# Three small edits to a two-layer graph kernel: a bias row's load behind x1's squares, one code step per tile step, and layer 0's slope on ScalarE

## The chip, the cores and the metric

The kernel runs on one core of one Trainium2 chip. The metric is the device time of one execution in microseconds (us); lower is better. A core has TensorE (PE, matmuls; its weight loads are listed as PEld), VectorE (DVE), ScalarE (ACT), GpSimd (POOL) and SyncE (SP). [...] Transfers are issued from the queues of SP, POOL and ACT[...].

## The reference

`x` is 4096 x 512, `adj` is a 4096 x 4096 matrix of 0 and 1 (int32).

```python
# layer 0
keep = (A > 0) & (cumsum(A > 0, axis=1) <= 64)        # at most 64 neighbours of a row
cnt  = keep.sum(axis=1, keepdims=True)
nb   = leaky_relu((keep @ X / max(cnt, 1)) @ W_nb.T + b_nb)        # slope 0.01
own  = leaky_relu(X @ W_line.T + b_line)
x1   = layernorm(X + own + where(cnt > 0, nb, 0))
# layer 1
Wh   = x1 @ W + bW
e    = leaky_relu((Wh @ a1 + b1)[:, None] + (Wh @ a2 + b2)[None, :], 0.2)
h    = softmax(where(adj > 0, e, -9e15), axis=1) @ Wh
out  = layernorm(x1 + h)
```

## The kernel before, in words

The 4096 rows are 32 blocks ("tiles") of 128. There is no scheduler: the order of the program's calls is the order in each engine's queue. Four stages follow each other.

**Stage 1** (L393 on) makes `y = X @ W_nb.T` (kept in SBUF as `y_hi + y_lo`) and the `own` part (to DRAM as `own_d`). Beside it run the **codes**: each row block of `adj` is cut in two chunks of 2048 columns, 64 chunks in all. For chunk q, `load_adj` fetches it on SP, `edge` (L167, ACT) turns it to 0/1 flags, `scan` (L179 to L184, DVE) counts down the 64 neighbours, and `pack` (L202 ACT, L203 a transfer on POOL) writes a byte code per edge to DRAM. Buffers of edge and left are two deep, so `edge(q+1)` waits until `scan(q-1)` is through.

**Stage 2** (L494 on) is `keep @ y`. Each of the 32 tiles is done in four steps of 8 blocks, so `s = 4 i + g` runs over 128 steps. One step on PE is 16 matmuls (L509, `y_hi` and `y_lo` in turn). `make_kt(s + 2)` (L249, ACT) unpacks the codes for two steps ahead into one of three `kt` buffers, which means that it waits for step s - 1 on PE. The codes of the second half of `adj` are still made here: `codes_step` at the end of a step starts a scan in 25 of 64 steps, and `codes_late` at the next step issues that chunk's `edge(q+1)` and `pack(q-1)` together.

`finish(i - 1, g)` ends the tile before, one part at each step: g = 0 scales the sum and adds the bias (L468) and applies the slope (L471), both on DVE; g = 1 adds `own` and starts the layer norm (L475, L117 to L126, the power on POOL); g = 2 applies it (L131) and stores x1 (L482); g = 3 makes the two dot products with `wa_rows` (L487).

**Stage 3** (L805 on) is `Wh = x1 @ W`, 32 steps of four matmuls each (L809). x1 comes from DRAM as 32 x 32 squares (`load_turned`, L561, SP) into four slots of the tile `front`, and `turn_x1` (L575, DVE) turns each to the matmul's layout; the first three go to the tile `early`, which lies where `y` lay. `finish_wh` (L584) adds the row `bias_w`; `combine_wh` (L597 to L600) makes sums of Wh that stage 4 wants. Beside it the attention weights of the first two blocks are made (`mask` L621 and L624, `score` L613, `weigh` L666), and `turn` (L685) and `combine` (L698 to L701) make the first two operands of stage 4. Ahead of the loop SP holds, in this order, W's four loads (L542), `bias_w` (L546), four `load_turned`, block 31's `own` (L777), the first `nat` codes (L608), and three more `load_turned`.

**Stage 4** (`consume`, L724) multiplies the weights with Wh by a scheme of seven products of blocks (Strassen), 64 calls over 16 pairs of blocks. Products 1 to 7 of a pair lie two to a PSUM bank, in an order `where` (L708); the very last call alone takes the products in another order (4, 1, 2, 6, 7, 5, 3). After it an epilogue (L876 to L896) joins the products, normalises and stores the last two blocks.

```python
            while late_q:
                q = late_q.pop()
                edge(q + 1)
                pack(q - 1)
...
                nc.vector.scalar_tensor_tensor(t, t, 0.01, t, ALU.mult, ALU.max)
...
    bias_w = ep.tile([P, C], F32, name="res", bufs=1)
    nc.sync.dma_start(bias_w, b_w.partition_broadcast(P))
```

Of the kernel before, what the change touches and what calls it, by code (L numbers as in the profile page):

```python
# [14 lines left out]
AF = mybir.ActivationFunctionType  # L15
ALU = mybir.AluOpType
# [4 lines left out]
P = 128  # L21
# [3 lines left out]
SLOPE = 0.01  # L25
# [7 lines left out]
def two_layer_adj_gnn(  # L33
# [16 lines left out]
    nc = tc.nc  # L50
    N, C = x.shape
    NB = N // P
# [84 lines left out]
    with ExitStack() as l0:  # L137
# [25 lines left out]
        def edge(s):  # L163
            if s < NB * NCH:
                b, h = divmod(s, NCH)
                edge_of[s] = adj_p.tile([P, CH], BF16, name="edge")
                nc.scalar.activation(  # L167
                    edge_of[s], loaded.pop(s), AF.Sigmoid, bias=steep[:, 0:1], scale=STEEP,
                    accum_out=cnts[:, h, b : b + 1],
                )  # L170
# [27 lines left out]
        def pack(s):  # L198
            if 0 <= s < NB * NCH:
                b, h = divmod(s, NCH)  # L200
                code = adj_p.tile([P, CH // 2], BF16, name="code")
                nc.scalar.copy(code.bitcast(U8), seen_of.pop(s))  # L202
                nc.gpsimd.dma_start(code_d[b][:, ts(h, CH // 2)], code)  # L203
# [16 lines left out]

        late_q = []

        def codes_late():

            while late_q:
                q = late_q.pop()
                edge(q + 1)
                pack(q - 1)

        def codes_step(s):  # L230
            while done[0] < min(s, NB * NCH + 1):
                codes_late()
                q = done[0]
                load_adj(q + 2)
                scan(q)
                late_q.append(q)
                done[0] += 1

        KB = 8
# [3 lines left out]
        def make_kt(s):  # L243
            if s < NB * NS:
                b, g = divmod(s, NS)
                if s not in kts:
                    kts[s] = ktb_p.tile([P, KB // 2, 2, P], F32R, name="kt")
                bytes_ = ktbs[b].bitcast(U8)[:, ts(g, KB // 2), :]
                nc.scalar.activation(  # L249
                    kts[s], bytes_.rearrange("p t (i r) -> p t r i", r=2),  # L250
                    AF.Sigmoid, bias=steep[:, 1:2], scale=STEEP,
                )
# [195 lines left out]

        def load_kt(b):
            if b < NB:  # L450
                assert done[0] > NCH * (b + 1) and not late_q
                ktbs[b] = ktb_p.tile([P, NT, P], BF16, name="ktb")
                nc.sync.dma_start_transpose(ktbs[b], code_d[b])

# [2 lines left out]
        def place(name, bufs=2):  # L457
# [2 lines left out]
                return spare.pop(0)  # L460
            return work.tile([P, C], F32, name=name, bufs=bufs)

        def finish(i, g):
            if i < 0:
                return
            if g == 0:
                t = place("t")
                nc.vector.scalar_tensor_tensor(  # L468
                    t, accs.pop(i), rcnt[:, i : i + 1], bias_nb, ALU.mult, ALU.add
                )  # L470
                nc.vector.scalar_tensor_tensor(t, t, 0.01, t, ALU.mult, ALU.max)  # L471
                fin[i] = t
            elif g == 1:
                t, y = fin[i], owns.pop(i)
                nc.vector.scalar_tensor_tensor(  # L475
                    y, t, some[:, i : i + 1], y, ALU.mult, ALU.add
                )
                fin[i] = y, ln_stats(y)
            elif g == 2:
                y, stats = fin[i]  # L480
                ln_apply(y, stats)
                nc.gpsimd.dma_start(x1_blk(i), y)  # L482
            else:
                y, _ = fin.pop(i)
                for k in range(2):
                    junk = place("junk", 1)
                    nc.vector.scalar_tensor_tensor(  # L487
                        junk, y, 1.0, wa_rows[k], ALU.mult, ALU.mult,
                        accum_out=e12[:, 1 - k, i : i + 1],
                    )  # L490
# [3 lines left out]
        for s in range(NB * NS):  # L494
            i, g = divmod(s, NS)
            make_kt(s + 2)
            codes_late()
            if g == 0:
                load_kt(i + 2)
                accs[i] = ps_acc.tile([P, C], F32, name="acc")  # L500
            if g == 2:
                if i < NB - 1:
                    owns[i] = place("own")
                    nc.sync.dma_start(owns[i], own_d[i])
            kt = kts.pop(s)
            for k in range(KB):
                j = g * KB + k
                for term in (y_hi, y_lo):
                    nc.tensor.matmul(  # L509
                        accs[i], kt[:, k // 2, k % 2, :], term[:, j, :],  # L510
                        start=(j == 0 and term is y_hi),
                        stop=(j == NB - 1 and term is y_lo),
                    )
            finish(i - 1, g)
            codes_step(start + int((s + 1) * RATE / NS))

# [24 lines left out]
            ws[ts(n, SQ), :, :], w[ts(n, P), :].rearrange("(m b) c -> b m c", b=SQ)  # L543
        )
    bias_w = ep.tile([P, C], F32, name="res", bufs=1)
    nc.sync.dma_start(bias_w, b_w.partition_broadcast(P))  # L546


    bt = big.tile([P, NS // 2, 7, HC], F32, name="bt")
# [6 lines left out]
    def load_turned(s):  # L556

        if s < NS:
            part = x1_d[s // 8].rearrange("(n s a) c -> s a n c", s=8, a=SQ)[s % 8]
            for n in range(NC):  # L560
                nc.sync.dma_start(  # L561
                    x1s[ts(n, SQ), s % 4, :].rearrange("a (j c) -> a j c", c=P),
                    part[:, :, ts(n, P)],
                )
# [37 lines left out]
    def load_nat(b, h):  # L602

        if b < NB:
            nats[b, h] = ep.tile([P, 2, NS * SQ // 2], BF16, name="nat")
            rows = code_d[b].rearrange("(i a) (n x) -> n a i x", a=SQ, n=4)
            for n in range(4):
                nc.sync.dma_start(nats[b, h][ts(n, SQ)], rows[n][:, ts(h, 2), :])  # L608
# [71 lines left out]
    def turn(q):  # L680

        g, k = divmod(q, NP)
        a = rp.tile([P, 2, 8, P], F32, name="a")
        for r in range(2):
            nc.vector.transpose(  # L685
                a[:, r].rearrange("p s (i a) -> p i s a", a=SQ),
                wts[2 * g + r][:, :, ts(k, 8 * SQ)].rearrange("p i (s x) -> p i s x", x=SQ),
            )
        if k == NP - 1:
            del wts[2 * g], wts[2 * g + 1]  # L690
        parts[q] = a
# [13 lines left out]
        }  # L705


    where = {1: (0, 0), 2: (0, 1), 4: (1, 0), 7: (1, 1), 5: (2, 0), 6: (2, 1), 3: (3, 0)}  # L708

    def consume(q):  # L710
        g, k = divmod(q, NP)
        if k == 0:
            two = [ps_s.tile([P, 2, HC], F32, name="pt")]
            two += [ps_acc.tile([P, 2, HC], F32, name="acc") for _ in range(3)]
            banks[g] = {n: two[i][:, j, :] for n, (i, j) in where.items()}
        part = parts.pop(q)


        order = (1, 2, 4, 7, 5, 6, 3) if q < NP * NT - 1 else (4, 1, 2, 6, 7, 5, 3)
        for n in order:  # L720
            lhs, rhs = part[n]
            mate = [m for m in order if where[m][0] == where[n][0]]
            for j in range(4):
                nc.tensor.matmul(  # L724
                    banks[g][n], lhs[:, j, :], bt[:, 4 * k + j, rhs, :],
                    start=(k == 0 and j == 0 and n == mate[0]),
                    stop=(k == NP - 1 and j == 3 and n == mate[-1]),
                )
# [46 lines left out]
    for s in range(4):  # L775
        load_turned(s)
    nc.sync.dma_start(owns[NB - 1], own_d[NB - 1])  # L777
    load_nat(0, 0)
    load_nat(0, 1)
    for s in range(3):  # L780
        turn_x1(s)
        load_turned(s + 4)
    for g in range(4):
        finish(NB - 1, g)


# [18 lines left out]
    for s in range(NS):  # L805
        pws[s] = ps_acc.tile([P, C], F32, name="acc")
        x1t = x1ts.pop(s)
        for m in range(NC):
            nc.tensor.matmul(  # L809
                pws[s], x1t[:, m, :], ws[:, m, :], start=(m == 0), stop=(m == NC - 1)  # L810
            )
        if s > 0:
            finish_wh(s - 1)
        turn_x1(s + 3)
        load_turned(s + 7)
        if FIRST <= s < FIRST + 8:
            b, i = divmod(s - FIRST, NI)
            mask(b, i)
            score(b, i)
        if FIRST + 4 <= s < FIRST + 12:  # L820
            b, i = divmod(s - FIRST - 4, NI)
            if i == 0:
                greatest(b)
                shift(b)
            weigh(b, i)
        if s in (FIRST + 14, FIRST + 18):
            q = (s - FIRST - 14) // 4
            turn(q)
            combine(q)
        elif s >= FIRST + 8:  # L830
            combine_wh()
    finish_wh(NS - 1)
# [98 lines left out]
```

## Time and profile before

| what | us |
|---|---|
| three runs | 1611.77, 1612.21, 1615.34 |
| median of the runs | 1612.21 |
| the profiled execution, its own time | 1611.63 |
| its span, first to last instruction | 1609.9 |
| stage 1's matmuls begin without a break | 84.4 |
| stage 2's matmuls | 235.7 to 704.2 |
| stage 3's matmuls | 709.7 to 826.1 |
| stage 4's matmuls | 826.1 to 1599.8 |

The profile is of one execution, taken by the hardware profiler. A group's line gives line, engine and operation, what it writes and reads, its shape and count, then the busy time and the mean duration in ns, then the engine's idle time before it and what ended that. The chain of waits follows the last instruction back, at each step to what released it. A timeline lists instructions by start and duration; the bracket behind one is the idle time of its engine before it. The windows view gives the engines' busy time in stretches, and the TensorE clock that was granted as a share of full speed.

### The profile page before, as it was taken

What the parts mean: (1) busy time and instruction counts of PE and PEld (TensorE: products, weight loads), DVE (VectorE), ACT (ScalarE), POOL (GpSimd) and SP (SyncE); (2) the same over time, 40 slices, a digit from 0 to 9 for tenths busy, and PEclk for the clock granted to TensorE, in tenths of its full rate; (3) what the DMA queues carried; (4) which work ended last, traced back from release to release, by engine and by line L of the source; (5) the groups of instructions that cost most, each with busy time, mean ns of one, the idle gap of its engine ahead of it and who ended that gap; (6) DMA issues with size and microseconds to landing.
All of it is one profiled execution on the core that took longest, in us unless ns stands there. A gap on an engine that the chain in (4) does not pass through costs nothing.

```text
span 1609.9 us, 18503 instructions
## 1 busy us (share of the span) xinstructions
PE 1583.8 (98%) x6456; PEld 1221.9 (76%) x6456; DVE 1328.1 (82%) x2186; ACT 903.2 (56%) x1054; POOL 258.1 (16%) x396
## 2 busy tenths in 40 slices
PE   9999999999999999989999999999999999999997
PEld 5444448888888787854468888888888888888886
DVE  4999987999999999845798788888788888788863
ACT  2655556677676766413437655567655567655520
POOL 4455532222122222101000000000000000000000
PEclk9999999999999999999999999999999999999999
DMA  8887868767776676335211111111111111111100
GB/s 199 286 264 232 262 211 239 216 202 212 220 208 198 209 213 193 100 103 118 79 40 27 53 40 53 44 29 46 53 41 53 43 30 47 53 40 53 40 7 33
DMA packets 168365, 192.74 MB, mean 120 GB/s; under 512 B 101408, under 2 KB 134464, under 8 KB 160080
## 3 DMA queue, kind: packets, MB, share of 16 engines
q1 hardware_dynamic: 147968, 131.38, 29.6%
q0 software_dynamic: 19728, 59.27, 10.8%
q8 instruction: 50, 0.82, 0.2%
q10 hardware_dynamic: 576, 0.92, 0.2%
q14 instruction: 43, 0.35, 0.1%
HBM read 132.65 MB, written 42.08 MB: 109 GB/s over the span
## 4 chain that ended last, share of the span: by engine, by line
PE 69%; DVE 23%; DMA 3%; issue 2%; ACT 1%; POOL 1%; SPq 0%; DVEq 0%; POOLq 0%; ACTq 0%
PE acc L724 34%; PE pt L724 14%; DVE left L179 10%; PE acc L340 9%; PE acc L509 9%; PE acc L809 3%; DVE left L184 2%; DVE junk L487 2%; DVE own L475 1%; DVE st L117 1%; DVE t L471 1%; DMA a<-in_adj_dram 1%; DVE t L468 1%; DVE own L131 1%; DVE c L575 1%
## 5 line engine op out<-in xcount | busy, mean ns | idle before, releaser
L509 PE MATMUL acc<-y_hi,kt 128*128 128x512 f32 x1016 | 396.3, 390 | 2.9 <-ACT kt L249 2.9
L509 PE MATMUL acc<-y_lo,kt 128*128 128x512 f32 x1016 | 395.8, 390 | 0.0
L724 PE MATMUL acc<-bt,s 128*128 128x256 f32 x1536 | 342.1, 379 | 0.0
L724 PEld LDWEIGHTS acc<-bt,s 128*128 128x128 f32 x1536 | 292.3, 190 | 39.2
L621 ACT ACTIVATE w<-nat,few 128x1024 f32<-128x1024 uint8 x128 | 136.9, 1135 | 277.1 <-DVE a L685 237.0
L126 POOL TENSOR_TENSOR rs<-ve,few 128x1 f32<-128x1 f32 x64 | 76.1, 1190 | 1021.1 <-DVE ve L124 1021.1
L724 PE MATMUL acc<-bt,a 128*128 128x256 f32 x1024 | 231.6, 379 | 0.0
L724 PE MATMUL pt<-bt,a 128*128 128x256 f32 x1024 | 231.5, 379 | 0.0
L509 PEld LDWEIGHTS acc<-y_hi,kt 128*128 128x128 f32 x1016 | 190.7, 188 | 44.5 <-ACT kt L249 5.0
L509 PEld LDWEIGHTS acc<-y_lo,kt 128*128 128x128 f32 x1016 | 190.9, 188 | 39.3
L724 PEld LDWEIGHTS pt<-bt,a 128*128 128x128 f32 x1024 | 194.9, 190 | 26.5 <-issue 0.5
L724 PEld LDWEIGHTS acc<-bt,a 128*128 128x128 f32 x1024 | 194.9, 190 | 26.1
L685 DVE STREAM_TRANSPOSE a<-w 128x1024 f32<-128x1024 f32 x128 | 153.0, 1225 | 56.1 <-ACT w L666 53.2
L249 ACT ACTIVATE kt<-ktb,few 128x1024 fp32r<-128x1024 uint8 x124 | 139.8, 1148 | 84.7 <-PE acc L509 69.0
L167 ACT ACTIVATE edge<-a,few 128x2048 bf16<-128x2048 int32 x64 | 127.9, 1998 | 99.4 <-DVE left L184 78.0
L613 ACT ACTIVATE w<-w,st_n 128x1024 f32<-128x1024 f32 x128 | 149.4, 1234 | 49.8 <-DVE m L624 49.8
L624 DVE CUSTOM_DVE_ANT_0 w<-e_n,w 128x1024 f32<-128x1024 f32 x128 | 149.5, 1221 | 9.1 <-ACT w L621 7.7
L666 ACT ACTIVATE w<-w,nm 128x1024 f32<-128x1024 f32 x128 | 145.4, 1137 | 11.3 <-DVE nm L657 11.3
L179 DVE TENSOR_TENSOR_SCAN left<-few,edge 128x2048 bf16<-128x2048 f32 x32 | 141.3, 4416 | 12.3 <-ACT edge L167 11.2
L179 DVE TENSOR_TENSOR_SCAN left<-few,ends,edge 128x2048 bf16<-128x2048 f32 x32 | 143.2, 4476 | 0.0
L202 ACT CAST code<-left 128x2048 uint8<-128x2048 bf16 x64 | 120.6, 1884 | 7.6 <-DVE left L184 7.6
L340 PE MATMUL acc<-wt_nb,xt 128*128 128x512 f32 x256 | 115.4, 594 | 1.8 <-DVE xt L294 1.0
(135 smaller groups left out, 1528.5 us busy)
## 6 DMA issues: line engine op xcount, KB each, us to landing
a<-in_adj_dram SPq DMA_DIRECT2D x64, 1024.0 KB, 5.7
code_d<-code POOLq DMA_DIRECT2D x64, 256.0 KB, 5.2
nat<-code_d SPq DMA_DIRECT2D x256, 64.0 KB, 2.0
own_d<-xb POOLq DMA_DIRECT2D x32, 256.0 KB, 5.7
w<-x_d SPq DMA_DIRECT2D x128, 64.0 KB, 2.0
c<-in_x_dram POOLq DMA_DIRECT2D x124, 64.0 KB, 5.5
xb<-in_x_dram POOLq DMA_DIRECT2D x31, 256.0 KB, 5.7
own<-own_d SPq DMA_DIRECT2D x31, 256.0 KB, 2.7
```

Source lines behind the costliest of these rows:

```text
L167: nc.scalar.activation(edge_of[s], loaded.pop(s), AF.Sigmoid, bias=steep[:, 0:1], scale=STEEP, accum_out=cnts[:, h, b : b + 1],)
L179: nc.vector.tensor_tensor_scan(left, two.to_broadcast([P, CH]), e, NEIGHBORS + 2.0 if h == 0 else end, ALU.max, ALU.subtract,)
L202: nc.scalar.copy(code.bitcast(U8), seen_of.pop(s))
L249: nc.scalar.activation(kts[s], bytes_.rearrange("p t (i r) -> p t r i", r=2), AF.Sigmoid, bias=steep[:, 1:2], scale=STEEP,)
L340: nc.tensor.matmul(pl, lhs_t[:, k, :], w_t[name][:, k, :], start=(k == 0), stop=(k == NC - 1),)
L509: nc.tensor.matmul(accs[i], kt[:, k // 2, k % 2, :], term[:, j, :], start=(j == 0 and term is y_hi), stop=(j == NB - 1 and term is y_lo),)
L613: nc.scalar.activation(dst, src, AF.Prelu, bias=bias, scale=scale, alpha=0.2)
L621: nc.scalar.activation(w_i, nats[b, i // 2].bitcast(U8)[:, i % 2, :], AF.Relu, bias=far, scale=-FAR)
L624: nc.vector.tensor_tensor_reduce(w_i, e2_n, w_i, 1.0, -3e38, ALU.subtract, ALU.max, m4s[b][:, i : i + 1])
L666: nc.scalar.activation(w_i, w_i, AF.Exp, bias=nms[b][:, i : i + 1], accum_out=z4s[g][:, r, i : i + 1])
L685: nc.vector.transpose(a[:, r].rearrange("p s (i a) -> p i s a", a=SQ), wts[2 * g + r][:, :, ts(k, 8 * SQ)].rearrange("p i (s x) -> p i s x ...
L724: nc.tensor.matmul(banks[g][n], lhs[:, j, :], bt[:, 4 * k + j, rhs, :], start=(k == 0 and j == 0 and n == mate[0]), stop=(k == NP - 1 and ...
```

## The change

It has five parts.

1. `bias_w`'s load (was L546) moves from ahead of the first four `load_turned` to behind the next three; the first `nat` loads move from ahead of the loop of stage 3 into its step 0, behind its `load_turned`.
2. `codes_late` issues one part at each step: `edge(q+1)` at the step after the scan, `pack(q-1)` at the one after that. A new scan, or a transfer of codes that needs it (`load_kt`), issues what is left.
3. The slope of layer 0 leaves DVE (L471) and becomes an activation (`Prelu`) on ACT, `bend0(i - 1)`, at step g = 2 behind `make_kt`. The parts of `finish` behind it come one step later: own and layer norm start at g = 2, x1 at g = 3, the dot products at g = 0 of the next tile.
4. The last pair of blocks uses the order (4, 1, 2, 6, 7, 5, 3) in all of its four calls, and its banks are paired by it: 4 with 1, 2 with 6, 7 with 5, 3 alone. Before, the pairs were 1 with 2, 4 with 7, 5 with 6 and 3 alone.
5. In stage 3 `turn` and `combine` of one operand stand two steps apart (steps 22, 24, 26, 28); before, both were in one step (22 and 26). `combine_wh` is left out at each of these steps, and what it left is done in the first call of stage 4.

```diff
-        def codes_late():
-
-            while late_q:
-                q = late_q.pop()
-                edge(q + 1)
-                pack(q - 1)
+        packed = [0]
+
+        def pack_late(q):
+            pack(q)
+            packed[0] = q + 1
+
+        def codes_late(n=1):
+
+            for part, q in late_q[:n]:
+                part(q)
+            del late_q[:n]
 
         def codes_step(s):
             while done[0] < min(s, NB * NCH + 1):
-                codes_late()
+                codes_late(2)
...
-                late_q.append(q)
+                late_q.extend([(edge, q + 1), (pack_late, q - 1)])
...
             if b < NB:
-                assert done[0] > NCH * (b + 1) and not late_q
+                if packed[0] < NCH * (b + 1):
+                    codes_late(2)
+                assert done[0] > NCH * (b + 1)
...
+        def bend0(i):
+            if i >= 0:
+                nc.scalar.activation(fin[i], fin[i], AF.Prelu, alpha=SLOPE)
...
-                nc.vector.scalar_tensor_tensor(t, t, 0.01, t, ALU.mult, ALU.max)
                 fin[i] = t
-            elif g == 1:
+            elif g == 2:
...
-            elif g == 2:
+            elif g == 3:
...
-            else:
+            elif g == 4:
...
             make_kt(s + 2)
+            if g == 2:
+                bend0(i - 1)
             codes_late()
...
+            if g == 0:
+                finish(i - 2, 4)
             finish(i - 1, g)
             codes_step(start + int((s + 1) * RATE / NS))
+        finish(NB - 2, 4)
...
-    nc.sync.dma_start(bias_w, b_w.partition_broadcast(P))
...
-    where = {1: (0, 0), 2: (0, 1), 4: (1, 0), 7: (1, 1), 5: (2, 0), 6: (2, 1), 3: (3, 0)}
+    order = {True: (1, 2, 4, 7, 5, 6, 3), False: (4, 1, 2, 6, 7, 5, 3)}
+    where = {key: {n: divmod(i, 2) for i, n in enumerate(o)} for key, o in order.items()}
...
-        order = (1, 2, 4, 7, 5, 6, 3) if q < NP * NT - 1 else (4, 1, 2, 6, 7, 5, 3)
-        for n in order:
+        key = g < NT - 1
+        for n in order[key]:
...
     nc.sync.dma_start(owns[NB - 1], own_d[NB - 1])
-    load_nat(0, 0)
-    load_nat(0, 1)
     for s in range(3):
         turn_x1(s)
         load_turned(s + 4)
-    for g in range(4):
+    nc.sync.dma_start(bias_w, b_w.partition_broadcast(P))
+    for g in range(5):
+        if g == 2:
+            bend0(NB - 1)
         finish(NB - 1, g)
...
         load_turned(s + 7)
+        if s == 0:
+            load_nat(0, 0)
+            load_nat(0, 1)
...
-        if s in (FIRST + 14, FIRST + 18):
-            q = (s - FIRST - 14) // 4
-            turn(q)
-            combine(q)
+        if s in range(FIRST + 14, FIRST + 22, 2):
+            q, part = divmod((s - FIRST - 14) // 2, 2)
+            (turn, combine)[part](q)
         elif s >= FIRST + 8:
             combine_wh()
```

More of the change, by code (lines that the diff above doesn't have):

```diff
@@ L714, in consume @@
             two += [ps_acc.tile([P, 2, HC], F32, name="acc") for _ in range(3)]
-            banks[g] = {n: two[i][:, j, :] for n, (i, j) in where.items()}
+            banks[g] = {n: two[i][:, j, :] for n, (i, j) in where[g < NT - 1].items()}
         part = parts.pop(q)
-        order = (1, 2, 4, 7, 5, 6, 3) if q < NP * NT - 1 else (4, 1, 2, 6, 7, 5, 3)
-        for n in order:
+        key = g < NT - 1
+        for n in order[key]:
             lhs, rhs = part[n]
-            mate = [m for m in order if where[m][0] == where[n][0]]
+            mate = [m for m in order[key] if where[key][m][0] == where[key][n][0]]
             for j in range(4):
```

## The prediction

> **What bounds the kernel now.** First the page's busy times, for what could be the bound at all:
>
> ```profile
> PE 1583.8 (98%) x6456; PEld 1221.9 (76%) x6456; DVE 1328.1 (82%) x2186; ACT 903.2 (56%) x1054; POOL 258.1 (16%) x396
> ```
>
> PE is the bound, and the span is its work plus its holes: 1609.9 - 1583.8 = 26 us are all that a change off PE can win, and an edit is worth what it does to a hole. The windows view says where they are (us of the stretch, then busy time of PE, PEld, DVE, ACT, POOL, the granted clock, DMA share, GB/s):
>
> ```profile
> 500.00:614.00 114.00, 111.10 (x486) 90.58 (x485) 108.20 (x134) 78.05 (x66) 28.63 (x29) 1.00 0.70 204
> ...
> 704.00:710.00 6.00, 0.53 (x2) 0.32 (x2) 0.81 (x2) 0.00 (x0) 0.00 (x0) 0.89 0.50 150
> 710.00:720.00 10.00, 10.00 (x18) 4.13 (x18) 6.03 (x12) 0.00 (x0) 1.14 (x2) 0.72 0.49 146
> ...
> 778.00:826.20 48.20, 45.49 (x106) 19.88 (x106) 45.62 (x98) 7.40 (x15) 0.00 (x0) 1.00 0.20 52
> ```
>
> Four places: late in stage 2, the passage to stage 3 at 704 (with a clock of 0.72 behind it, so busy time hides a loss there too), late in stage 3, and the end after stage 4. Between them PE has no hole (826 to 1598 is all busy). The chain of waits (start, us, what) says who made the first two:
>
> ```profile
> 608.36 1.78 issue
> 610.14 0.19 ACT edge L167
> 610.33 1.11 ACT code L202
> ...
> 612.02 1.15 ACT kt L249
> 613.17 0.04 issue
> 613.22 91.01 PE acc L509 x400
> 704.23 0.14 SPq L546
> ...
> 705.83 2.97 DMA w<-x_d
> ...
> 708.92 0.72 DVE w L575
> ...
> 709.69 44.37 PE acc L809 x96
> ```
>
> At 613 PE waits for kt, which stands on ACT behind an edge that DVE's scan held up (in ACT's timeline it waited 4.52 us for L184) and behind a 1.88 us pack. At 704 the bias row L546 heads SP's queue, issued only when stage 2's last matmuls are done; x1's squares wait behind it, though they go where W's loads had gone at 680. Then 3 us of transfer, a transpose, and PE starts at 709.69. Its clock shows in the weight loads' starts:
>
> ```profile
> 710.70 0.34 PEld L809 LDWEIGHTS acc<-w 128*128 128x128 f32 x1 [0.52 <-issue]
> 711.55 0.34 PEld L809 LDWEIGHTS acc<-w 128*128 128x128 f32 x1 [0.52 <-issue]
> ...
> 716.11 0.19 PEld L809 LDWEIGHTS acc<-w 128*128 128x128 f32 x1 [0.24 <-issue]
> 716.54 0.19 PEld L809 LDWEIGHTS acc<-w 128*128 128x128 f32 x1 [0.24 <-issue]
> ```
>
> 0.85 apart at first, 0.43 later: half speed until 715.7.
>
> **Part 1, the loads, on the path.** With the row gone from their front the squares of x1 can be issued from about 682 and land during stage 2. The transpose L575 does not move as far: in the program built from the change the first transpose writes `early`, which waits for stage 2's second last matmul. SP's L546 waited for that same one and went at 704.02, so the transpose runs 704.05 to 704.76 and PE starts near 704.85 instead of 709.69: 4.85 won. The hole shrinks to 0.8 us. Stage 3's own holes of 1.1 to 3.3 us between weight loads are followed by loads 0.43 apart, so the clock should stay up. The ninth weight load came at 715.68; at 0.43 from 709.68 it is 713.11: 2.57 more. [...] I take the row, 2.6.
>
> What is queued behind: DVE does block 31's finish next, 6.1 to 13.0 us after 704 by its rows (L468 0.71, slope 0.63 plus two hand-overs, L475 to L124 1.8, POOL 0.75, L131 0.55, dot products 1.2, L788 to L794 0.8), then the transpose of step 3 at 713.8; PE wants it at 704.85 + 3 x 3.43 = 715.1. The row itself goes at about 710.5 (own load 0.4, twelve square loads of 0.47) and with its 3.6 us lands at 714.1, when finish_wh(0) is due at 713.8: 0.3 us on DVE, which has some 3 before step 4 at 718.6. The nat codes land near 722; mask's result is first used about 737. All hidden; the cost if not is 0.4 to 2 us once.
>
> **Part 5, late stage 3.** Weight loads stand 1.36 and 3.26 apart at 777 and 781, and 1.15 at 818. The first two come from ACT and DVE handing masks to each other, which stays. The third is DVE: 781 to 818 without a pause, with turn and combine in one step (2.33 + 2.74). The change takes two times combine_wh (1.66 each) and combine(1) (2.7) from ahead of that transpose: 1.15 - 0.43 = 0.7 won. Two combine_wh more then fall to stage 4's first call, before turn(2). By DVE's rows combine(2) now ends at 848.5 of before's clock instead of 846.5, and PE wants it at 850.2. It fits by less than 2 us; cost 0 to 1, I take 0.
>
> **Part 4, the end.** The epilogue's first sum (L877) reads products 1 and 6, and waited for 5, the mate of 6:
>
> ```profile
> 1598.14 0.42 DVE L877 TENSOR_TENSOR c<-c,acc 128x256 f32<-128x256 f32 x1 [19.49 <-PE acc L724]
> ```
>
> Now 6 comes with 2, one product after another of 1.73 us: L877 and L878 can run two products earlier. L879 wants 7, whose mate is 5, so it starts at 1598.14 instead of 1598.93: 0.8 won. The rest is DVE's chain, unchanged.
>
> **Parts 2 and 3, stage 2.**
>
> ```profile
> L374 ACT ACTIVATE t<-t 128x512 f32<-128x512 f32 x32 | 20.0, 626 | 48.0 <-DVE t L370 48.0
> L471 DVE SCALAR_TENSOR_TENSOR t<-t 128x512 f32<-128x512 f32 x31 | 21.5, 692 | 1.1
> L167 ACT ACT_TABLE_LOAD x1 | 1.3, 1283 | 0.0
> ```
>
> The slope leaves DVE (0.69, 0.72 from start to start) and costs ACT 0.63 per tile. L374 is the same activation in stage 1, on the same tile shape. [...] The row decides: in stage 1 edge's sigmoid and this activation alternate, with one load at the first edge and none after. The price is zero.
>
> What it buys: the start of L468 trails the end of its tile on PE by 4.0 us at tile 1 and 14.3 at tile 17 (268.4 and 510.8 in the timeline), so a tile costs DVE 242.4 / 16 = 15.15, and PE 64 x 0.2266 = 14.5. DVE falls behind 0.65 per tile until edge, held by DVE, holds kt. From tile 18 on PE's weight loads show six gaps (525 to 631), together 4.8 us over their spacing; stage 2 has no other. Without the slope 15.15 - 0.72 = 14.43, just under 14.5: the lag no longer grows.
>
> New waits: on ACT bend0 waits for L468, with the next edge or pack and then kt of the next step behind it; on DVE L475 waits for bend0, with all scans behind it. bend0 stands behind make_kt, which waits for PE's step 1 of the tile: so L475 starts no sooner than 7.25 + 1.15 + 0.63 + 0.15 = 9.2 after the tile before has ended. One scan of 5.75 more or less between two L475 moves that by +2.4 (two scans) or -3.3 (one); in the program's pattern never more than two twos follow, so L475 trails by 9.2 to 14.1. L468 then trails by 0 to 10, below the 14.6 at which the first gap came; bend0, reached 8.4 after the tile's end, waits at most about 2, and kt has some 6 in hand. A pack no longer stands between edge and kt (1.88 at 610). Bounds: 4.8 won if all gaps go, nothing if the new waits leave as many, a loss below. Nearest to the numbers is nearly all: 4.3.
>
> **Sum.** 4.85 + 2.6 + 0.7 + 0.8 + 4.3 = 13.2. Profiled execution 1611.6 - 13.2 = 1598.4; the median of the runs is 0.6 above it, so 1598.9. (A measurement here tells about 0.2%, 3 us, from no change.)
>
> **Rivals.** *Stage 2's gaps stay*, because DVE, at 14.43 of 14.5, also waits for L475's floor: its margin of 0.07 speaks for it, the bounded lag against. Then 8.95 is won: 1603.3. *The clock falls all the same* or a load in the passage is late: 2.6 less, 1601.5. *The squares still do not come early*: a wait at SP that I missed, so that this part of the change does not do what it says; W's loads at 680 in front of them speak against. Without the 7.45 of the passage: 1606.3, and with stage 2's gaps left as well 1610.6, no change. *Slower:* ACT and DVE go in lockstep. bend0 waits for DVE, kt behind it starves PE, and PE's delay moves the next floor. It decides from (8.95 + 4.8) / 31 = 0.44 us of PE wait per tile; at 0.7 it is 21.7 instead of 4.8: 1612.2 - 8.95 + 16.9 = 1620.2. Against it: ACT would have to wait 6 us at bend0 before PE notices.
>
> **Chances.** As forecast 0.65 (1596.5 to 1601); stage 2 unchanged 0.16; clock or load 0.08; no early squares 0.02, with stage 2's gaps left as well 0.03; lockstep 0.06. So faster 0.91, same 0.03, slower 0.06. The range, 1595.5 to 1605, takes in the first three: from all gaps gone with a little of the mask holes, to stage 2 unchanged with 1.7 us more lost.
>
> **What would show it.** PE's first L809 at 704.8 to 705 with weight loads 0.43 apart at once and a clock of 1.00 in 704 to 720; square loads on SP near 682; no gap over 1 us between L509; a steady lag of L479 (the old L468); no table load beside the four; L895 (the old L877) about 5.1 before the last product's end instead of 1.6. Wrong would be: gaps of L509 with "ACT kt" waiting behind the Prelu, or a hole at the start of stage 4.

## The result, and the profile after

| | before | after |
|---|---|---|
| median of five runs, us | 1612.91 | 1600.41 |
| lowest to highest, us | 1611.77 to 1615.34 | 1599.35 to 1601.63 |
| profiled execution, its own time, us | 1611.63 | 1600.12 |
| its span, us | 1609.9 | 1598.4 |

The change makes the kernel faster by 0.8%: the ratio of the times is 0.9922, with a 95% interval of 0.9908 to 0.9936. The forecast was 1598.9, so the time is 1.5 us above it and inside the range of 1595.5 to 1605.

The page's busy times, after:

```profile
PE 1579.6 (99%) x6456; PEld 1218.4 (76%) x6456; DVE 1305.4 (82%) x2154; ACT 924.2 (58%) x1086; POOL 260.0 (16%) x396
```

ACT has 32 instructions more and DVE 32 fewer, and 22.7 us of DVE's busy time went against 21.0 more on ACT. PE still bounds the kernel. The windows view of after, in the stretches where before had its holes (columns as in the prediction: PE, PEld, DVE, ACT, POOL, granted clock, DMA share, GB/s; the last two rows are 3.4 us each):

```profile
500.00:614.00 114.00, 114.00 (x505) 94.39 (x504) 106.20 (x132) 86.27 (x78) 27.30 (x27) 1.00 0.71 215
...
704.00:710.00 6.00, 6.00 (x15) 2.66 (x14) 4.13 (x14) 0.56 (x2) 2.41 (x4) 1.00 0.51 163
710.00:720.00 10.00, 10.00 (x24) 4.37 (x23) 5.65 (x9) 1.15 (x1) 3.83 (x8) 1.00 0.81 130
...
769.40:772.80 3.40, 1.17 (x3) 0.30 (x2) 3.30 (x9) 3.23 (x5) 0.00 (x0) 1.00 0.00 0
772.80:776.20 3.40, 3.40 (x5) 1.35 (x4) 3.30 (x8) 1.40 (x4) 0.00 (x0) 0.50 0.28 80
```

Stage 2 has no hole left (114.00 of 114 us, before 111.10), and the passage from stage 2 to stage 3 has 1.19 us between weight loads instead of 6.08, and no low clock. The last two rows are what the prediction did not have: the hole late in stage 3 (the "late hole" from here on), which the change does not touch, is followed by 3.4 us at half clock. In before the same hole was followed by full clock:

```profile
780.40:783.80 3.40, 1.71 (x4) 0.41 (x3) 2.41 (x7) 3.17 (x8) 0.00 (x0) 1.00 0.13 36
783.80:787.20 3.40, 2.85 (x7) 1.42 (x8) 3.33 (x8) 2.36 (x6) 0.00 (x0) 1.00 0.27 78
```

The chain of waits of after, from 560 to 720, has shrunk to five pieces:

```profile
559.94 139.87 PE acc L521 x617
...
699.83 0.72 DVE w L589
...
700.60 19.58 PE acc L825 x45
```

The edges and the kt of before, its SP piece and its transfer are gone; only the transpose (L589) stands between the stages, 0.72 us long. The weight loads behind it:

```profile
700.60 0.30 PEld L825 LDWEIGHTS acc<-w 128*128 128x128 f32 x2 [1.00 <-DVE w L589]
701.13 0.19 PEld L825 LDWEIGHTS acc<-w 128*128 128x128 f32 x1 [0.24 <-issue]
```

Each of the single loads behind the first pair starts 0.19 + 0.24 = 0.43 after the one before: full speed at once, with a granted clock of 1.00 in the rows above. Among the groups, the slope on ACT and the addition of `own` on DVE that waits for it:

```profile
L472 ACT ACTIVATE t<-t 128x512 f32<-128x512 f32 x31 | 19.1, 615 | 1.0 <-DVE t L479 0.9
L485 DVE SCALAR_TENSOR_TENSOR own<-t,e,own 128x512 f32<-128x512 f32 x31 | 23.2, 749 | 26.3 <-ACT t L472 26.2
```

The slope costs ACT 0.615 us a tile. Over these 31 tiles ACT waits 0.9 us in all for its sum and DVE 26.2 us in all for the slope; stage 2 has no gap, so neither costs PE anything. The program has four table loads of 1.28 us, as before. In the epilogue the first sum, in DVE's timeline:

```profile
1584.02 0.42 DVE L895 TENSOR_TENSOR c<-c,acc 128x256 f32<-128x256 f32 x1 [16.03 <-PE acc L739]
```

The last product ends at 1589.1, so L895 stands 5.1 ahead of it, as worked out, instead of 1.6.

**Where the 11.5 us of span went**, between marks in the two traces (starts of PE's weight loads, since the ends of matmuls are modelled):

| stretch | before | after | won | foreseen |
|---|---|---|---|---|
| stage 2, first to last weight load | 468.47 | 464.22 | 4.25 | 4.3 |
| last load of stage 2 to the first of stage 3 | 6.08 | 1.19 | 4.89 | 4.85 |
| from there to stage 3's ninth load | 6.00 | 3.11 | 2.89 | 2.6 |
| gap at 818 (before) | 1.15 | none | 0.39 | 0.7 |
| last load of stage 4 to the end | 10.68 | 9.84 | 0.84 | 0.8 |
| half clock behind the hole late in stage 3 | none | 3.4 us | -1.69 | 0 |

The sum is 11.57, against 1609.86 - 1598.35 = 11.51; stage 2 began 0.06 later. The gap at 818 and the half clock lie in one stretch, from stage 3's ninth load to stage 4's first, which took 109.95 before and 111.26 after. They are parted with the help of a kernel below that has neither (edge and pack together, 109.57): 0.39 won by the gap, 1.69 lost by the clock. Stage 2's 464.2 has no gap left in it: after's weight loads there stand 0.227 apart (median), and 2048 at the prediction's 0.2266 are 464.1. Stage 4 is the same in both traces, 773.5.

### The profile page after: what moved, and what is told of

The parts are those of the page before. It is cut to its first block, busy times and chain, and to the rows that moved or that the text cites. A ratio compares the mean times of both kernels' runs of the same rounds, so it can differ in the third digit from the quotient of the medians.

```text
span 1598.4 us, 18483 instructions
## 1 busy us (share of the span) xinstructions
PE 1579.6 (99%) x6456; PEld 1218.4 (76%) x6456; DVE 1305.4 (82%) x2154; ACT 924.2 (58%) x1086; POOL 260.0 (16%) x396
## 4 chain that ended last, share of the span: by engine, by line
PE 92%; DVE 3%; DMA 2%; issue 1%; ACT 1%; SPq 0%; POOL 0%; DVEq 0%; POOLq 0%; ACTq 0%
PE acc L739 34%; PE acc L521 29%; PE pt L739 14%; PE acc L345 9%; PE acc L825 5%; DMA c<-in_x_dram 1%; DVE left L179 1%; DMA a<-in_L_gnn_W_line_dram 1%; DMA edge<-in_L_gnn_a_dram 0%; DVE edge L361 0%; DVE xt L299 0%; DMA w<-x_d 0%; DVE y_lo L435 0%; DVE t L375 0%; ACT w L635 0%
## 5 line engine op out<-in xcount | busy, mean ns | idle before, releaser
L167 ACT ACTIVATE edge<-a,few 128x2048 bf16<-128x2048 int32 x64 | 127.4, 1991 | 43.4 <-DVE left L184 20.3
L680 ACT ACTIVATE w<-w,nm 128x1024 f32<-128x1024 f32 x128 | 145.4, 1136 | 11.3 <-DVE nm L671 11.3
```

Of the source, the lines that this page charges most:

```text
L167: nc.scalar.activation(edge_of[s], loaded.pop(s), AF.Sigmoid, bias=steep[:, 0:1], scale=STEEP, accum_out=cnts[:, h, b : b + 1],)
L680: nc.scalar.activation(w_i, w_i, AF.Exp, bias=nms[b][:, i : i + 1], accum_out=z4s[g][:, r, i : i + 1])
```

## The experiments

The theory after the result: the slope on ACT emptied stage 2, with nothing from the parting of edge and pack; the order of SP's queue closed the passage; the banks and the turns did the small rest; and the forecast was 1.5 us off because a hole's price is not only its length but what the clock does behind it. The main rivals: parting edge and pack emptied stage 2, or both were needed; and the half clock late in stage 3 comes from the new orders of parts 2 to 5, not from chance. All times below are medians. The first set (the row first, the slope on DVE, both back, flags with fill) had before at 1614.45 (1613.06 to 1615.72, nine runs), the second at 1612.15 (1611.63 to 1613.18, nine runs). The start of stage 2 differs from run to run by up to 3 us (235.1 to 238.2 in the traces), so the readings rest on stretches between marks.

**The bias row first again.** The change with its row back in front of x1's squares:

```diff
     bias_w = ep.tile([P, C], F32, name="res", bufs=1)
+    nc.sync.dma_start(bias_w, b_w.partition_broadcast(P))
...
-    nc.sync.dma_start(bias_w, b_w.partition_broadcast(P))
```

> The changed kernel with bias_w's load put back ahead of x1's squares, all else as changed. If the row at the head of SP's queue made the passage's hole: stage 3's first weight load comes about 6.1 us after stage 2's last (1.2 in the changed kernel), the next ones stand 0.85 apart for some 6 us, and the time is 4.9 + 2.9 = 7.8 us over the changed kernel, near 1608. If the row is not the cause (the squares would wait for something else, or the half clock has another cause), it stays within 2 us of 1600.4.

Measured: 1607.85 (1606.77 to 1608.86), ratio to before 0.9958 (0.9946 to 0.9971). SP's timeline, with the row at L561:

```profile
701.81 0.35 SPq L561 DMA_DIRECT2D res<-in_L_gnn_bW_dram  x1
```

and PE's weight loads:

```profile
707.07 0.50 PEld L825 LDWEIGHTS acc<-w 128*128 128x128 f32 x2 [5.49 <-DVE w L590]
708.08 0.34 PEld L825 LDWEIGHTS acc<-w 128*128 128x128 f32 x1 [0.52 <-issue]
```

In after the squares' transfers were already being issued from 674 and the row only at 706.95; here they follow the row at 702. The gap between the stages is 5.68 (after: 1.19), and loads stand 0.85 apart until 713.1. Stage 2 stays at 464.2. So the row's place in the queue makes the hole of the passage and the half clock behind it, 4.49 for the gap and 2.97 for the clock, and touches nothing else. The hole is 0.4 shorter than in before (6.08), as the squares took 2.56 to land here and 2.97 there; why is not shown. From stage 2's last load to stage 4's first it takes only 5.75 more than in after, because in this run the late hole, 3.25 long as ever, was not followed by half clock (1.00 from 777.9 to 784.7): 4.49 + 2.97 - 1.70, to rounding. That the time met the expected 1608 all the same is luck: stage 2 began 2.0 us later than in after.

**The slope on DVE again.** Every other part stays, finish too is one step later:

```diff
+                nc.vector.scalar_tensor_tensor(t, t, 0.01, t, ALU.mult, ALU.max)
                 fin[i] = t
...
-            if g == 2:
-                bend0(i - 1)
...
-        if g == 2:
-            bend0(NB - 1)
```

> The changed kernel with the slope of layer 0 on DVE again (behind the bias, at g = 0), the parts of a code step still apart. If the slope on DVE is what lets DVE fall behind: DVE's lag at L479 grows again by some 0.6 us per tile to over 14, gaps between stage 2's weight loads come back with 3 to 5 us together, and the time is 1603.5 to 1605.5. Rival, that the parting of edge and pack removed the gaps: the lag grows, but the gaps stay under 1 us, and the time stays near 1600.5.

Measured: 1605.55 (1604.24 to 1606.0), ratio 0.9942 (0.993 to 0.9955). Stage 2 takes 468.4, which gives back 4.17 of the 4.25. It does so in another place: two gaps, 0.69 at 574 and 2.47 at 592. The sum of a tile (L479) starts about 4 to 9 us behind the end of its tile on PE at tiles 2 to 7 in this kernel and in after, and 13.2 to 16.6 behind it at tiles 22 to 26 here, against 3.2 to 7.9 in after. The chain of waits of this kernel, ahead of the second gap:

```profile
585.14 0.70 DVE t L482
585.84 0.23 SPq L515
...
586.17 6.92 DMA a<-in_adj_dram
...
593.62 0.19 ACT edge L167
593.80 1.05 ACT kt L254
594.89 5.31 PE acc L520 x15
```

DVE's lag reaches PE by a way that the prediction did not have: SP's load of `own` (L515) waits for the late DVE, the next rows of `adj` stand behind it in the queue and then take 6.92 us, edge waits for them, kt stands behind edge, and PE waits for kt. Its windows:

```profile
591.60:595.00 3.40, 1.54 (x8) 0.97 (x6) 3.16 (x11) 3.29 (x4) 0.48 (x1) 1.00 1.05 186
595.00:598.40 3.40, 3.40 (x9) 2.62 (x10) 3.40 (x1) 3.40 (x3) 3.40 (x1) 0.50 0.77 292
```

Half clock follows this gap too, at some 1.5 us. So of the 4.17 only 2.7 are gaps, and that the sum comes so near to before's 4.25, where no half clock followed, is chance.

**Edge and pack together, the slope on ACT.** One default argument:

```diff
-        def codes_late(n=1):
+        def codes_late(n=2):
```

> The changed kernel with edge and pack issued together again (the slope stays on ACT). With the slope off DVE, DVE does not fall behind, so stage 2 should stay at 471.5 to 472.5 and the time at that of the changed kernel; if the parting of the two matters by itself, 1 to 2 us of gaps come back (it was worth 1.1 with the slope on DVE).

Measured: 1598.73 (1598.56 to 1601.01), ratio 0.9919 (0.9906 to 0.9933). Stage 2 takes 464.2, with no gap, and L485 trails its tile by 9.5 to 14.9 (after: 9.5 to 14.5). So in the change the parting of edge and pack is worth nothing. That the median lies 1.7 below the change's own in the same set is the clock, as the windows of this kernel around the late hole show:

```profile
768.80:772.20 3.40, 1.61 (x4) 0.38 (x2) 2.52 (x7) 3.17 (x8) 0.00 (x0) 1.00 0.10 29
772.20:775.60 3.40, 2.96 (x7) 1.44 (x8) 3.33 (x8) 2.25 (x4) 0.00 (x0) 1.00 0.27 77
```

The hole is as long as in after (3.25 between weight loads), but it falls over two windows, with 1.8 of 3.4 us idle in the first (after: 2.2), and the clock stays at 1.00. The mean granted clock of the timed runs agrees: 0.998 in the four of 1598.56 to 1599.17 and 0.997 in the one of 1601.01, while of the change's five runs in this set four have 0.997.

**Both back.** The two edits above together:

```diff
-        def codes_late(n=1):
+        def codes_late(n=2):
...
+                nc.vector.scalar_tensor_tensor(t, t, 0.01, t, ALU.mult, ALU.max)
                 fin[i] = t
...
-                bend0(i - 1)
...
-            bend0(NB - 1)
```

> As the one with the slope on DVE, and edge and pack issued together again: stage 2 as before but for the later parts of finish. Both theories of stage 2 expect the gaps back, 4 to 5 us together from tile 18 on, and about 1604.6. If neither slope nor parting matters (the later finish alone did it), it stays near 1600.4.

Measured: 1607.09 (1606.14 to 1608.53), ratio 0.9954 (0.9942 to 0.9967). Stage 2 takes 469.5, with five gaps of 0.63 to 2.48 between 463 and 634 and no half clock (the trace's mean clock is 0.997, as in after, where the half clock late in stage 3 is the only one ahead of the last product). What this stage 2 still has of the change is the later finish, which therefore did not empty it. The parting saves about 1.1 us of stage 2 where DVE lags (469.5 against 468.4, one trace each), by gaps alone some 2.6 (5.3 against 2.7), and nothing where it does not. The time is 2.5 above the expected 1604.6; in the trace stage 2 lost 5.3 instead of some 4.2, and began 3.05 later than in after.

**The banks and the turns as before.** Parts 4 and 5 undone: the banks paired by the old `where`, `turn` and `combine` in one step:

```diff
-    order = {True: (1, 2, 4, 7, 5, 6, 3), False: (4, 1, 2, 6, 7, 5, 3)}
-    where = {key: {n: divmod(i, 2) for i, n in enumerate(o)} for key, o in order.items()}
+    where = {1: (0, 0), 2: (0, 1), 4: (1, 0), 7: (1, 1), 5: (2, 0), 6: (2, 1), 3: (3, 0)}
...
-        if s in range(FIRST + 14, FIRST + 22, 2):
-            q, part = divmod((s - FIRST - 14) // 2, 2)
-            (turn, combine)[part](q)
+        if s in (FIRST + 14, FIRST + 18):
+            q = (s - FIRST - 14) // 4
+            turn(q)
+            combine(q)
```

> The changed kernel with the last pair's banks as before and turn and combine in one step again. The end of the last product to the end of the span is 10.7 instead of 9.8 (0.8 more), and a gap of 1.1 between weight loads comes back before step 30 of stage 3, worth 0.4 to 0.7 on PE's path. If the turns do not matter there, the gap stays away. Together 1.2 to 1.5 us, to be read in the trace and not in the time.

Measured in a single run: 1600.08, no different from the change's 1600.44. The trace says why: the tail is 10.70 instead of 9.84 and the gap of 1.16 is back at 806, worth 0.4, together 1.26; but the late hole has no half clock behind it (mean clock 0.998; after 0.997), 1.69 the other way. That the time comes out even is chance.

**The change once more**, unaltered, to see whether the half clock comes again:

> The changed kernel once more, unaltered, beside the others of this set. Its ratio to before should be 0.9922 within 0.0015. In the trace stage 2 from first to last weight load takes 471.5 and the last product to the end 9.8. [...]

Measured: 1600.44 (1600.32 to 1602.12), ratio 0.993 (0.9917 to 0.9942). The hole is 3.25 long and half clock follows (mean clock 0.997); stage 2 takes 464.2 and the tail 9.85. (The 471.5 in this expectation and in an earlier one counts from an entry 7.3 us ahead of the first load, which is a wait.) Both traces of the change have the half clock, and so has the kernel with the slope on DVE (0.57 from 779 to 783); the one with the row first, which keeps parts 2 to 5 as well, has not. So these parts by themselves are not its cause. What goes with it in the traces is how long PE stood idle in the 3.4 us ahead of it (2.23 in after, 1.70 in the row first); the last section has the numbers, and no edit shows this as the cause.

**The flags one step ahead.** If the late holes come from ACT and DVE handing masks to each other, ACT's half of `mask` made one step earlier takes them away:

```diff
-    def mask(b, i):
+    def flags(b, i):
...
+    def masked(b, i):
...
+            if s == FIRST:
+                flags(0, 0)
+            if s < FIRST + 7:
+                flags(*divmod(s + 1 - FIRST, NI))
             b, i = divmod(s - FIRST, NI)
-            mask(b, i)
+            masked(b, i)
```

> The changed kernel with flags issued one step ahead and nothing between greatest and shift. If the handing to and fro of masks alone made both holes, they are under 1 us as in the one with combine_wh between as well, and the time is the same within 1 us, 4 to 5 us under the changed kernel. If the wait for ACT behind greatest has its own share, a hole of 1 to 2 us stays at step 19.

A second kernel does the same and puts a `combine_wh` between the two steps of DVE that are left over at the end of the masks:

```diff
+                if s >= FIRST + 8:
+                    combine_wh()
...
-        elif s >= FIRST + 8:
+        elif s > FIRST + 8:
```

> The changed kernel with the holes of late stage 3 filled: the activation of mask (flags) is issued one step ahead of its DVE part, so that ACT does the next flags while DVE takes the greatest, and one combine_wh stands between greatest(1) and shift(1). If DVE and ACT handing masks to each other made the holes (1.38 and 3.25 between weight loads, 3.8 over the spacing) and the long one the half clock behind it (2.0): both holes under 1 us, no loads 0.85 apart, 5 to 6 us less than the changed kernel: near 1595. Rival, that DVE's own work is too much there: the hole moves and 0 to 2 us are won.

Measured: the flags alone 1595.84 (1595.68 to 1596.94), ratio 0.9899 (0.9886 to 0.9913); with the fill 1597.19 (1596.45 to 1598.23), ratio 0.9891 (0.9876 to 0.9906) in the first set. From stage 2's last weight load to stage 4's first both take 110.73, after 115.56: 4.83 won, and the fill adds nothing. (The second kernel misses the expected 1595; in its trace stage 2 begins at 238.1, against 235.7 in the first's.) PE's timeline with the flags ahead:

```profile
701.16 10.57 PE L832 MATMUL acc<-w 128*128 128x512 f32 x24 [0.58 <-DVE w L589]
711.57 99.73 PE L832 MATMUL acc<-w,c 128*128 128x512 f32 x232
```

and the same stretch of after:

```profile
711.00 55.10 PE L825 MATMUL acc<-w,c 128*128 128x512 f32 x128
766.46 3.70 PE L825 MATMUL acc<-w,c 128*128 128x512 f32 x8 [0.36 <-DVE c L589]
772.39 43.16 PE L825 MATMUL acc<-w,c 128*128 128x512 f32 x96 [2.23 <-DVE c L589]
```

One unbroken run of 232 matmuls stands where after has two breaks, so the late holes do come from the masks. This version beats both kernels: in the set that has both, 1595.84 against the change's 1600.44. The 4.83 is more than the 3.8 by which the two holes exceed the spacing of loads, because the 1.69 of half clock goes with them.

## Why the prediction was right, and where it was off

**Part 1, the loads: right.** "PE starts near 704.85 instead of 709.69: 4.85 won" was 4.89. The transpose does stop at stage 2's last matmuls, as the chain shows (L589 between the two stages). The clock behind the passage was taken from the row at 2.6; removing it won 2.89, and the kernel with the row first lost 2.97. The row was the right choice: half speed lasted 6.83 us there (708.71 to 715.54 in before). The rest of 0.3 is the first pair of weight loads: they stand 0.11 apart in place of 0.43. The row landed later than worked out and made DVE wait 1.52 (L598) instead of 0.3, hidden as said.

**Parts 2 and 3, stage 2: right in size and in main cause, one link wrong.** The slope's 0.69 a tile on DVE is what made the lag grow; without it the lag stays, L479 at 0.5 to 8.8 and, the last two tiles aside, L485 at 9.5 to 14.5 (worked out: 0 to 10 and 9.2 to 14.1). "The price is zero" held for ACT's tables: the trace has the same four loads as before, of 1.28 us each (L150, L167, L808, L680), and none in stage 2. "A pack no longer stands between edge and kt" has no share of its own: with edge and pack together stage 2 is as short. And a lagging DVE does not only hold edge by its scan, it holds SP by `own` as well (L515 at 585.84 with the slope on DVE, right behind DVE's L482).

**Part 4: right**, 0.84 for 0.8. Undone, the tail is 10.70 again. L895 had no part in the tail's length; what counts is L897, which waited for PE until 1587.41 and heads DVE's chain to the end.

**Part 5: right in sign, the size off.** 0.39 instead of 0.7. The gap was read between weight loads, 1.15 - 0.43. But behind the late hole of after the first two loads stand 0.11 apart (772.39 and 772.50) in place of 0.43, so part of the gap between loads is made good. Undone in the experiment, the gap was worth 0.4 too. This 0.3 too much and the 0.3 too little for the clock of the passage cancelled in the sum, so that the sum came out so near is in part luck.

**The step that was wrong** is this one: "Stage 3's own holes of 1.1 to 3.3 us between weight loads are followed by loads 0.43 apart, so the clock should stay up." It held in before (loads 0.43 apart from 784.89 on), and for the new hole of the passage, for which it was used (0.43 from 701.13 on). It did not hold in after for stage 3's own holes, for whose clock the working had no term: the unchanged hole of 3.25 cost 1.69 more in after. Without that loss the measured 11.57 would have been 13.26, against 13.2 worked out. The runs show it from both sides: where the hole had no half clock behind it, edge and pack together ran at 1598.73, and the change itself, with it in both its traces, at 1600.41 and 1600.44.

**The rivals.** *Stage 2's gaps stay*: no, all six went. *The clock falls all the same*: it fell, but at another hole than the one named. *The squares do not come early*: they were issued from 674. *Lockstep of ACT and DVE*: DVE did wait 26.2 us for the slope, in 10 waits of up to 8.3, but ACT only 0.9 us for DVE's sums, so the loop never closed.

## What to carry to other kernels

Read an off-path engine's work per tile against the bound engine's period: 0.65 us too much per tile, unseen for 17 tiles, was worth 4.25 us, and taking 0.72 of 15.15 us a tile off that engine ended it. A transfer that must wait for late work belongs behind those that could go early: in SP's queue here the squares went from 702.2 behind the row, which had waited until 701.81, and from 674.33 without it. When all holes but a few are gone, those few can have a price twice over, in their length and in the clock: the late hole of after was 3.25 us between weight loads, and the half clock behind it took 1.69 more. So close them (here by handing over one step earlier, worth 4.83) rather than count on the clock.

## What the runs showed of the hardware

The traces of before and after record when the granted clock changed. In after it was full for 768.0 us (from the record's first entry, 4.82, to 772.82), half for 3.413 and full for 815.8 (to 1592.02); in before it was full for 699.7 (from 8.98 to 708.71), half for 6.827 and full for 887.5 (to 1603.00). Each is a whole multiple of the shortest, to 0.02 us: 225, 1 and 239, and 205, 2 and 260. Half speed lasted 3.4 us with the slope on DVE too (595.0 to 598.4), and 6.8 with the row first (706.2 to 713.0).

In these traces the outcome goes with how long PE stood idle in the 3.4 us ahead, and not with the length of the hole. The windows below end where the clock changed or, where it stayed, a whole number of 3.413 us from a change in the same trace; that of edge and pack together is the one shown with its run. The ends of matmuls are modelled, so the idle times have some tenths of play:

| PE idle in the window, us | kernel and window | granted clock behind it |
|---|---|---|
| 3.41 | before, passage, 705.30 to 708.71 | 0.50 for 6.8 us |
| 3.40 | the row first, passage, 702.8 to 706.2 | 0.50 for 6.8 us |
| 2.23 | after, late hole, 769.41 to 772.82 | 0.50 for 3.4 us |
| 1.86 | the slope on DVE, stage 2's second gap, 591.6 to 595.0 | 0.50 for 3.4 us |
| 1.79 | edge and pack together, late hole, 768.8 to 772.2 | 1.00 |
| 1.74 | before, stage 2's gap at 611, 609.72 to 613.13 | 1.00 |
| 1.70 | the row first, late hole, 777.9 to 781.3 | 1.00 |
| 1.69 | before, late hole, 780.39 to 783.80 | 1.00 |

In these eight windows half clock came behind 1.86 us of idle PE and more, full clock behind 1.79 and less. The two lie closer than the play of the numbers, so where the one turns into the other is not shown. A late hole of the same 3.25 us was followed by half clock in four traces of eight, which in after cost 1.69, and of the two gaps of 2.4 to 2.5 us in these rows from stage 2 only one was (the slope on DVE, at 592).

The two passages differ in two ways from the two other holes with half clock behind them, as the row first shows:

```profile
702.80:706.20 3.40, 0.00 (x0) 0.00 (x0) 0.00 (x0) 0.00 (x0) 0.00 (x0) 1.00 0.66 192
706.20:713.00 6.80, 5.93 (x7) 2.52 (x8) 2.77 (x4) 1.83 (x2) 0.00 (x0) 0.50 0.48 121
```

PE was idle for the whole of the first window, and again for 0.9 of the 6.8 us at half clock (in before 1.0), while in the 3.4 us of half clock in after, and of that in stage 2 with the slope on DVE, it was busy throughout (3.41 of 3.41, 3.40 of 3.40). Which of the two made the half clock last twice as long is not shown.

No run moved a hole against these windows with all else the same: that idle time within them decides the clock is my conjecture from the eight rows above, and no edit shows it. Edge and pack together, an edit that touches nothing near the late hole, ran 1.7 us below the change in the same set, with a clock of 1.00 behind that hole. Whether this is chance in each run, or in part set by the kernel, is open: of the change's ten timed runs eight have a mean clock of 0.997, of the five with edge and pack together one.
